# Attention projections of six units per block as seven products of halves

## The chip, the cores and the metric

The kernel runs on one core of a Trainium2 chip. The core has a matrix engine (TensorE; PE in the profile, with PEld for its weight loads), VectorE (DVE), ScalarE (ACT), GpSimd (POOL), and SyncE (SP), whose queue issues the transfers between the device memory and the core's SBUF. Matmuls write to eight banks of PSUM. The metric is the device time of one execution in microseconds.

## The reference

Thirty-two sequences of 64 positions with 512 features, in fp32, go through two layers. Each is conditioned by its own row of `cond`. Cut to what matters:

```python
# layer 0: 8 query heads of 64, one key/value head
h = ada_rms(x, cond, ln1_w, ln1_tw)              # normed, scaled per sequence
q, k = rope(h @ Wq.T), rope(h @ Wk.T);  v = h @ Wv.T
x = x + softmax(q @ k.T / 8) @ v @ Wo.T          # Wq, Wo: 512 x 512
h = ada_rms(x, cond, ln2_w, ln2_tw)
x = x + (silu(h @ Wg.T) * (h @ Wu.T)) @ Wd.T     # 512 -> 2048 -> 512
# layer 1: 16 query heads of 32, four key/value heads from a latent of 128
h = ada_layernorm(x, cond, W_ada, b_ada)
q = rope(h @ Wq.T);  c = h @ Wkd.T;  k, v = rope(c @ Wku.T), c @ Wvu.T
x = x + softmax(q @ k.T / sqrt(32)) @ v @ Wo.T   # Wq, Wo: 512 x 512
```

The mask of layer 1 hides nothing at 64 positions.

## The kernel before

The 2,048 positions are cut into eight units of 256 (four sequences). Everything is kept transposed: features on the partitions, positions along the columns, so a unit of `x` is four chunks of 128 features by 256 positions. There are three kinds of work for a unit: `attention0`, `mlp` and `attention1`.

The MLP already multiplies by halves: a 256x256 block of weights times a 256x256 block of a unit, cut in two both ways, takes seven products of halves in place of eight (Strassen's scheme in Winograd's form, P1 to P7). `first_products` makes P1, P6, P5, P7 in the four parts of a PSUM bank; VectorE and ScalarE read them into sums; `last_products` makes P2, P3, P4 over parts of the same bank. A set of weights holds seven 128x256 pieces, three quarters of the weights and four sums (`set`, 896 KB). The sums are made in unit 0 (`combine`, L250) and stored to device memory (`kept`); later units load both parts (L242 and L247) into a ring of five sets. The loads are issued when the last products of a set have been emitted (`done_with`).

The attention projections are whole products. `project` (L523) runs over the four chunks: a unit's queries or outputs are 4 x 4 multiplications of 128 features by 256 positions. In both blocks `query(0)` and `query(1)` make two chunks each and `rotate` (L527) applies the positional rotation straight from PSUM; `output` (L564) projects the contexts `cT` and VectorE adds the result to `x` (L573). Their weights (`wqkv`, `wo0`, `wq1`, `wo1`) stay in SBUF throughout, in the fixed area of 14,103 columns (`STAY`).

Two pools of PSUM matter: attention has two banks ("at"), the MLP two for gate and up ("gu") and four for down.

The order of the work is made in two steps. A planner (`Order`, L67) emits pieces of generators: each piece yields its PE cost and a latency before its successor may come, and the job with the smallest share done goes first. During the MLP of unit u run `attention0` of unit u + 1 and, from unit 1 on, a chain of `attention1` of earlier units (`behind`, L1058). The framework then places each engine's instructions by readiness, with that order as priority; so instructions of different pieces are interleaved, and each engine's order is fixed when the program is built. Units 0 and 1 of block 0, and 6 and 7 of block 1 (at the end), run with `lean`, a variant with less latency; the other six units of each block do not.

Of the kernel before, what the change touches and what calls it, by code (L numbers as in the profile page):

```python
# [17 lines left out]
P = 128  # L18
# [29 lines left out]
STAY = 14103  # L48
# [60 lines left out]
def two_blocks(ctx: ExitStack, tc: tile.TileContext, a: dict, out: bass.AP):  # L109
# [115 lines left out]


# [38 lines left out]

    mods = []
# [16 lines left out]
    for i, w in enumerate(wqkv):  # L283
        nc.sync.dma_start(w, a[f"wqkv{i}"])
# [238 lines left out]
    def project(ps, w, cols, h):  # L523
        for k in range(KC):
            nc.tensor.matmul(ps, w[:, k, cols], h[:, k, :], start=(k == 0), stop=(k == KC - 1))  # L525

    def rotate(dst, src, cos, sin, shape, name):  # L527
# [7 lines left out]
        nc.vector.stream_shuffle(v, v, OTHER)  # L535
        nc.gpsimd.tensor_tensor(dst, u, v, ALU.add)  # L536
# [27 lines left out]
    def output(u, cT, w, name, last=False):  # L564

        x = x_units[u]
        for h in range(2):
# [12 lines left out]
    def attention0(u, room, early=None, late=None):  # L580
# [4 lines left out]
        def query(i):  # L585

            q = abank(f"q0_{u}_{i}").rearrange("p (c t) -> p c t", c=2)
            for c in range(2):
                project(q[:, c], wqkv[i], slice(c * P, (c + 1) * P), h)
# [8 lines left out]
        def keys_values():  # L598
            kv = abank(f"kv0_{u}")
            project(kv[:, :UT], wqkv[0], slice(2 * P, 3 * P), h)  # L600
            return kv

        norm = rms(u, s0a, h, room, f"a{u}")
        yield next(norm)
# [19 lines left out]
        turn = turn or query(0)  # L624
        turn(cos, sin)
        yield 0.0 if lean else 3.4, 0.0
# [22 lines left out]
        query(1)(cos, sin)  # L649
        yield 3.4, 0.0  # L650
# [14 lines left out]
        for ts in ((0,), (1,)) if lean else ((0, 1),):  # L665
# [16 lines left out]
            yield 0.5 * len(ts), 5.0 * ts[0] if lean else 10.0  # L682
# [56 lines left out]
        yield 0.43, 0.0  # L739


    def attention1(u, room):
# [6 lines left out]
        else:  # L749
# [4 lines left out]
            yield 0.0, 6.0  # L754
            mean = mean_of([total], f"mean_{u}")
        sq = tile4(room, "h", f"sq1_{u}") if lean else work("sq", [P, KC, UT], f"sq1_{u}", 1)
        for part in (slice(0, 2), slice(2, 4)) if lean else (slice(0, 4),):
# [3 lines left out]
            nc.scalar.activation(sq[:, part], h[:, part], AF.Square)  # L761
        parts = [sq[:, k] for k in range(KC)] if lean else [total_of(room, sq, f"v{u}")]
# [7 lines left out]
        for part in (slice(0, 2), slice(2, 4)) if lean else (slice(0, 4),):  # L770
# [7 lines left out]
        project(lat[:, :UT], wkd, slice(0, LAT), h)  # L778
# [7 lines left out]
        def query(i):  # L786
            q = abank(f"q1_{u}_{i}")
            for c in range(2):
                project(q[:, c * UT : (c + 1) * UT], wq1, slice((2 * i + c) * P, (2 * i + c + 1) * P), h)
# [10 lines left out]
        query(0)  # L800
        yield 3.4, 0.0
# [31 lines left out]
        query(1)  # L833
        yield 3.4, 4.5
# [24 lines left out]
        def context(t, ps):  # L859
# [19 lines left out]
            yield 1.0, 1.5 * t  # L879
# [315 lines left out]
```

## Time and profile before

| What | Value |
|---|---|
| median of 3 runs | 1057.65 us (1056.87 to 1057.7) |
| the profiled execution | 1055.26 us, of which span 1053.4 us |
| granted PE clock over the span | 0.989 |
| PE busy, PE weight loads busy | 96%, 89% |
| VectorE, ScalarE, GpSimd busy | 52%, 31%, 41% |
| moved by DMA | 198.55 MB, 188 GB/s in the mean |
| query projections, records of 256 columns (L525 `q`) | 512 |
| output projections (L525 `po`) | 512 |
| gate and up products of 128 columns (L899) | 3584 |

The profile is one execution with the hardware profiler. Instructions are grouped by line, engine and tile names (buffer numbers left out); the chain of work follows the end of the program back to what released each step. Matmuls are pipelined and their ends are modelled, so durations of single matmuls overlap; the distance from one to the next is read from the chain.

### The profile page before, as it was taken

To read this page: it belongs to the slowest core of one execution; us is meant where nothing else is said; L and a number is where in the kernel's file an instruction comes from. 1 tells how busy PE (TensorE), PEld (TensorE's weight loads), DVE (VectorE), ACT (ScalarE), POOL (GpSimd) and SP (SyncE) were. 2 spreads that over 40 slices of the span, in tenths; PEclk is the share of its full clock that TensorE was granted. 3 is DMA by queue.
4 is the path that set the end of the run, shared out by engine and by line. 5 is a ranking of instruction groups with operands and counts; after the bars stand their busy time and mean duration, and the time that the engine had idled before them with its cause. 6 is when DMAs were issued, how large, how long until landed. Compare 5 with 4: busy or idle time off the path is not lost.

```text
span 1053.4 us, 21591 instructions
## 1 busy us (share of the span) xinstructions
PE 1012.6 (96%) x8602; PEld 938.7 (89%) x8602; DVE 546.7 (52%) x1377; ACT 329.1 (31%) x680; POOL 432.8 (41%) x518
## 2 busy tenths in 40 slices
PE   7899999999999999999999999999999999999887
PEld 6679999998999889989999989999999899999765
DVE  4966646545355385353555286532655345352363
ACT  4342112255114243142431332341424422141132
POOL 3424545443255443355341544234632335432541
PEclk8989999999999999999999999999999999999899
DMA  8816896463666364663555565465735547564001
GB/s 277 310 61 218 288 303 247 151 211 122 234 210 211 108 244 152 219 243 127 212 178 181 207 209 183 141 214 187 277 117 194 202 165 280 204 229 170 11 1 40
DMA packets 68275, 198.55 MB, mean 188 GB/s; under 512 B 7248, under 2 KB 15184, under 8 KB 67792
## 3 DMA queue, kind: packets, MB, share of 16 engines
q1 hardware_dynamic: 68176, 197.17, 53.4%
q8 instruction: 69, 1.13, 0.4%
q14 instruction: 30, 0.25, 0.1%
HBM read 180.37 MB, written 16.78 MB: 187 GB/s over the span
## 4 chain that ended last, share of the span: by engine, by line
PE 81%; DVE 8%; POOL 5%; DMA 2%; issue 2%; ACT 1%; SPq 0%; ACTq 0%; POOLq 0%; DVEq 0%
PE gu L899 34%; PE down L958 17%; PE po L525 10%; PE q L525 9%; DMA set<-in_wmlp 2%; PE cx L869 2%; PE sc L845 1%; PE lat L525 1%; PE pp L560 1%; PE sc L673 1%; PE kv L525 1%; PE cx L694 1%; DVE sm L553 1%; PE tab L400 1%; DVE mx L545 1%
## 5 line engine op out<-in xcount | busy, mean ns | idle before, releaser
L899 PE MATMUL gu<-h,set 128*128 128x128 f32 x2048 | 288.1, 277 | 6.4 <-DVE c L918 5.7
L899 PEld LDWEIGHTS gu<-h,set 128*128 128x128 f32 x2048 | 258.8, 192 | 15.5 <-issue 10.4
L899 PE MATMUL gu<-hc,set 128*128 128x128 f32 x1536 | 215.2, 275 | 0.0
L899 PEld LDWEIGHTS gu<-hc,set 128*128 128x128 f32 x1536 | 193.5, 192 | 1.0 <-issue 0.6
L937 POOL TENSOR_TENSOR act<-c,c 128x384 f32<-128x384 f32 x64 | 66.4, 1038 | 210.5 <-DVE c L925 140.8
L958 PE MATMUL down<-td,set 128*128 128x128 f32 x1024 | 137.5, 276 | 3.3 <-POOL td L940 2.5
L958 PEld LDWEIGHTS down<-td,set 128*128 128x128 f32 x1024 | 125.4, 192 | 5.2 <-POOL td L940 3.5
L911 ACT COPY e<-gu 128x128 f32<-128x128 f32 x128 | 33.7, 264 | 259.9 <-PE gu L899 246.8
L525 PE MATMUL q<-h,stays 128*128 128x256 f32 x480 | 111.3, 385 | 1.5 <-POOL h L774 1.5
L525 PE MATMUL po<-cT,stays 128*128 128x256 f32 x480 | 109.0, 382 | 2.1 <-DVE sm L553 2.1
L958 PE MATMUL down<-act,set 128*128 128x128 f32 x768 | 109.5, 278 | 0.0
L925 DVE TENSOR_TENSOR c<-gu,u 128x256 f32<-128x256 f32 x128 | 53.4, 419 | 106.4 <-PE gu L899 106.1
L525 PEld LDWEIGHTS q<-h,stays 128*128 128x128 f32 x480 | 90.9, 193 | 14.3 <-POOL h L774 1.7
L525 PEld LDWEIGHTS po<-cT,stays 128*128 128x128 f32 x480 | 89.8, 191 | 14.0 <-ACT cT L878 2.6
L958 PEld LDWEIGHTS down<-act,set 128*128 128x128 f32 x768 | 97.6, 192 | 5.2 <-issue 3.2
L913 DVE TENSOR_TENSOR u<-e,gu 128x128 f32<-128x128 f32 x128 | 35.9, 281 | 127.5 <-ACT e L911 126.8
L555 POOL TENSOR_TENSOR p<-p,sm 128x512 f32<-128x512 f32 x40 | 41.6, 1058 | 121.4 <-DVE sm L554 113.7
L536 POOL TENSOR_TENSOR qT<-u_q,v_q 128x512 f32<-128x512 f32 x30 | 38.1, 1269 | 97.2 <-DVE v_q L535 97.1
L573 DVE TENSOR_TENSOR x<-x,po 128x512 f32<-128x512 f32 x32 | 22.0, 687 | 87.7 <-PE po L525 87.7
L994 ACT ACT_TABLE_LOAD x34 | 43.6, 1283 | 54.5 <-DVE c L925 54.0
L939 POOL TENSOR_TENSOR td<-act 128x256 f32<-128x256 f32 x64 | 46.7, 730 | 5.6 <-DVE act L936 0.9
L994 ACT ACTIVATE c<-gu 128x128 f32<-128x128 f32 x64 | 17.7, 277 | 90.2 <-DVE c L925 82.2
(269 smaller groups left out, 1333.0 us busy)
## 6 DMA issues: line engine op xcount, KB each, us to landing
set<-sums SPq DMA_DIRECT2D x168, 512.0 KB, 5.6
set<-in_wmlp SPq DMA_DIRECT2D x192, 384.0 KB, 4.6
sums<-set SPq DMA_DIRECT2D x24, 512.0 KB, 4.1
x<-in_x SPq DMA_DIRECT2D x8, 512.0 KB, 5.5
out_x<-x SPq DMA_DIRECT2D x16, 256.0 KB, 2.3
mod<-in_mod SPq DMA_DIRECT2D x7, 512.0 KB, 5.2
a<-in_wmlp SPq DMA_DIRECT2D x24, 128.0 KB, 3.1
stays<-in_wo SPq DMA_DIRECT2D x2, 1024.0 KB, 8.0
```

The source lines that it names most:

```text
L525: nc.tensor.matmul(ps, w[:, k, cols], h[:, k, :], start=(k == 0), stop=(k == KC - 1))
L536: nc.gpsimd.tensor_tensor(dst, u, v, ALU.add)
L555: nc.gpsimd.tensor_tensor(p8, p8, sm.unsqueeze(2).to_broadcast(wide), ALU.mult)
L573: nc.vector.tensor_tensor(x[:, part], x[:, part], po, ALU.add)
L899: nc.tensor.matmul(ps, w[:, slot, k * P : (k + 1) * P], b[of][:, k], start=start and k == 0, stop=k == 1, skip_group_check=True)
L911: nc.scalar.copy(e, ps[:, 0])
L913: nc.vector.tensor_tensor(u2, e, ps[:, 1], ALU.add)
L925: nc.vector.tensor_tensor(c.rearrange("p (a b) t -> p a b t", b=2)[:, :, 1], ps[:, 2:4], u2.unsqueeze(1).to_broadcast([P, 2, HT]), ALU.add,)
L937: nc.gpsimd.tensor_tensor(act[:, 1:4], gate[:, 1:4], c[:, 1:4], ALU.mult)
L939: nc.gpsimd.tensor_tensor(td[:, 0:2], act[:, 1:3], act[:, 0:2], ALU.subtract)
L958: nc.tensor.matmul(sums_of[u][p][:, c], w[:, slot, c * P : (c + 1) * P], b[of], start=q % NP == 0 and i % 2 == 0 and c == 0, stop=q % NP = ...
L994: nc.scalar.activation(gate[2][:, 0], gate[0][:, 0], AF.Silu)
```

## The change

Non-lean units, six in each block, make their query and output projections by seven products of halves. `load_asets` loads a pair of sets per projection (`wattn`, `akept`), two rings of two, one for each block; the next pair is asked for where the last projection has been emitted. In the first unit of each block `combine_asets` makes the four weight sums of each set and stores them. `sums_in` makes the four sums of the input on VectorE: for queries as soon as the norm has made `h`, for outputs just ahead of the products. `in_halves` makes the products of both sets, evacuates them into `c` in SBUF, and leaves the rest to `rotate`, or to GpSimd, which adds `c` to `x`. Lean units keep the whole products: the first two from tiles that are dropped afterwards, the last two from weights loaded ahead of the last unit's MLP into the tiles of block 0's ring. Some costs and latencies that the planner is given change with it.

```diff
-STAY = 14103
+STAY = 5911
...
-    wqkv = [fixed([P, KC, 384]), fixed([P, KC, 256])]
-    wo0 = fixed([P, KC, D])
-    wq1 = fixed([P, KC, D])
+    wkv0 = fixed([P, KC, P])
+    wq0 = [work("wq0", [P, KC, 2 * P], f"wq0_{i}") for i in range(2)]
+    wo0 = work("wo", [P, KC, D], "wo0", 1)
     wkd = fixed([P, KC, LAT])
     wkv1 = fixed([P, 2, P])
-    wo1 = fixed([P, KC, D])
+    whole1 = []
...
+    def by_chunk(w):
+        return [w[:, k] for k in range(KC)]
+    def product(ps, p, w, b, start=False, stop=False):
+        slot, of = OF[p]
+        for k in range(2):
+            nc.tensor.matmul(
+                ps, w[:, slot, k * P : (k + 1) * P], b[of][:, k], start=start and k == 0, stop=k == 1, skip_group_check=True
+            )
...
+    akept = [dram.tile([P, 4, 2 * P], F32, tag=f"asums{i}", name=f"asums{i}") for i in range(8)]
+    asets = {b: {"n": 0, "now": [], "odd": [], "units": 6} for b in range(2)}
+    def load_asets(block):
+        s_ = asets[block]
+        n = s_["n"]
+        if n == 2 * s_["units"]:
+            return
+        s_["n"], s_["now"], s_["odd"] = n + 1, [], []
+        for i in range(2):
+            j = 4 * block + 2 * (n % 2) + i
+            t = work(f"aw{block}", [P, 7, 2 * P], f"aset{block}_{n}_{i}", 2)
+            nc.sync.dma_start(t[:, 4:7], a["wattn"][j][:, 0:3])
+            if n < 2:
+                s_["odd"].append(work("a21", [P, 2 * P], f"aa21_{block}_{n}_{i}", 2))
+                nc.sync.dma_start(s_["odd"][-1], a["wattn"][j][:, 3])
+            else:
+                nc.sync.dma_start(t[:, 0:4], akept[j])
+            s_["now"].append(t)
+    def combine_asets(block):
+        s_ = asets[block]
+        for i, a21 in enumerate(s_["odd"]):
+            t = s_["now"][i]
+            nc.vector.tensor_tensor(t[:, 0], a21, t[:, 6], ALU.add)
+            nc.vector.tensor_tensor(t[:, 1], t[:, 0], t[:, 4], ALU.subtract)
+            nc.vector.tensor_tensor(t[:, 2], t[:, 4], a21, ALU.subtract)
+            nc.gpsimd.tensor_tensor(t[:, 3], t[:, 5], t[:, 1], ALU.subtract)
+            nc.sync.dma_start(akept[4 * block + 2 * ((s_["n"] - 1) % 2) + i], t[:, 0:4])
+        s_["odd"] = []
+    def sums_in(block, h, name):
+        t = work(f"as{block}", [P, 4, 2, HT], f"as_{name}", 1)
+        b11, b12, b21, b22 = (h[:, r_, c_] for r_ in (slice(0, 2), slice(2, 4)) for c_ in (slice(0, HT), slice(HT, UT)))
+        nc.vector.tensor_tensor(t[:, 0], b12, b11, ALU.subtract)
+        nc.vector.tensor_tensor(t[:, 2], b22, b12, ALU.subtract)
+        nc.vector.tensor_tensor(t[:, 1], b22, t[:, 0], ALU.subtract)
+        nc.vector.tensor_tensor(t[:, 3], b21, t[:, 1], ALU.subtract)
+        return {"B11": b11, "B21": b21, "B22": b22, "T1": t[:, 0], "T2": t[:, 1], "T3": t[:, 2], "T4": t[:, 3]}
+    def in_halves(block, b, name):
+        some = []
+        for i, w in enumerate(asets[block]["now"]):
+            ps = abank(f"ha_{name}_{i}").rearrange("p (r t) -> p r t", t=HT)
+            for j, p in enumerate(("P1", "P6", "P5", "P7")):
+                product(ps[:, j], p, w, b, start=j == 0)
+            e = work("ea", [P, HT], f"ea_{name}_{i}")
+            nc.scalar.copy(e, ps[:, 0])
+            u2 = work("u2a", [P, HT], f"u2a_{name}_{i}")
+            nc.vector.tensor_tensor(u2, e, ps[:, 1], ALU.add)
+            w2 = work("w2a", [P, HT], f"w2a_{name}_{i}")
+            nc.vector.tensor_tensor(w2, u2, ps[:, 2], ALU.add)
+            c = work("ca", [P, 4, HT], f"ca_{name}_{i}")
+            nc.vector.tensor_tensor(c[:, 3], w2, ps[:, 3], ALU.add)
+            some.append((w, ps, u2, c))
+        for w, ps, u2, c in some:
+            for j, p in ((0, "P2"), (2, "P3"), (3, "P4")):
+                product(ps[:, j], p, w, b, stop=p == "P4")
+            nc.scalar.copy(c[:, 0], ps[:, 0])
+            nc.vector.tensor_tensor(c[:, 1:3], ps[:, 2:4], u2.unsqueeze(1).to_broadcast([P, 2, HT]), ALU.add)
+        return [c.rearrange("p (r c) t -> p r (c t)", r=2) for _, _, _, c in some]
+    def pair_of(t, i):
+        return t.rearrange("p (r i) t -> p i r t", r=2)[:, i]
...
-    for i, w in enumerate(wqkv):
-        nc.sync.dma_start(w, a[f"wqkv{i}"])
+    nc.sync.dma_start(wkv0, a["wkv0"])
+    for i, w in enumerate(wq0):
+        nc.sync.dma_start(w, a[f"wq0{i}"])
...
-            nc.tensor.matmul(ps, w[:, k, cols], h[:, k, :], start=(k == 0), stop=(k == KC - 1))
+            nc.tensor.matmul(ps, w[k][:, cols], h[:, k, :], start=(k == 0), stop=(k == KC - 1))
...
+        if list(dst.shape) != list(u.shape):
+            u, v = (t.rearrange("p (r b) s -> p r (b s)", r=2) for t in (u, v))
         nc.gpsimd.tensor_tensor(dst, u, v, ALU.add)
...
     def output(u, cT, w, name, last=False):
 
         x = x_units[u]
+        if w is None:
+            block = int(last)
+            for i, c in enumerate(in_halves(block, sums_in(block, cT, f"o{name}"), f"o{name}")):
+                nc.gpsimd.tensor_tensor(pair_of(x, i), pair_of(x, i), c, ALU.add)
+                if last:
+                    nc.sync.dma_start(pair_of(out[u], i), pair_of(x, i))
+            yield 6.3, 2.0
+            return
...
-        yield next(norm)
+        at_first = next(norm)
+        if not lean:
+            combine_asets(0)
+            h_sums = sums_in(0, h, f"q0_{u}")
+        yield at_first
...
-        turn = turn or query(0)
-        turn(cos, sin)
-        yield 0.0 if lean else 3.4, 0.0
+        if lean:
+            turn(cos, sin)
+            yield 0.0, 0.0
...
-        query(1)(cos, sin)
-        yield 3.4, 0.0
+        if lean:
+            query(1)(cos, sin)
+            yield 3.4, 0.0
+        else:
+            two = [P, 2, UT]
+            for i, c in enumerate(in_halves(0, h_sums, f"q0_{u}")):
+                rotate(
+                    pair_of(qT, i), c, *(t.unsqueeze(1).to_broadcast(two) for t in (cos, sin)), two, f"q0_{u}_{i}"
+                )
+            yield 6.3, 0.0
+            load_asets(0)
...
-            yield 0.5 * len(ts), 5.0 * ts[0] if lean else 10.0
+            yield 0.5 * len(ts), 5.0 * ts[0] if lean else 12.5
+        if not lean:
+            combine_asets(0)
...
             contexts([0, 1])
-            yield 1.1, 2.5
-        yield from output(u, cT, wo0, f"0_{u}")
+            yield 1.1, 4.0
+        yield from output(u, cT, by_chunk(wo0) if lean else None, f"0_{u}")
...
         if late:
             late()
         yield 0.43, 0.0
+        if not lean:
+            load_asets(0)
...
             yield 0.0, 6.0
+            if u:
+                load_asets(1)
...
             nc.scalar.activation(sq[:, part], h[:, part], AF.Square)
+        if not lean:
+            combine_asets(1)
...
             nc.gpsimd.tensor_tensor(by_seq(h[:, part]), by_seq(h[:, part]), per_seq(t1, u)[:, part], ALU.add)
+        if not lean:
+            h_sums = sums_in(1, h, f"q1_{u}")
         yield 0.43, 5.5 if lean else 9.0
...
-        query(1)
-        yield 3.4, 4.5
+        if lean:
+            query(1)
+            yield 3.4, 4.5
+        else:
+            many = [P, 2 * US, S]
+            for i, c in enumerate(in_halves(1, h_sums, f"q1_{u}")):
+                rotate(
+                    pair_of(qT, i),
+                    c.rearrange("p r (b s) -> p (r b) s", s=S),
+                    cos.unsqueeze(1).to_broadcast(many),
+                    sin.unsqueeze(1).to_broadcast(many),
+                    many,
+                    f"q1_{u}_{i}",
+                )
+            yield 6.3, 4.5
+            load_asets(1)
...
-            yield 1.0, 1.5 * t
+            yield 1.0, 1.5 * t if lean else 3.5 * t
...
-            yield 0.9, (0.0, 6.0)[t] if lean else 9.0
+            yield 0.9, (0.0, 6.0)[t] if lean else 11.5
             if not lean:
+                combine_asets(1)
                 yield from context(t, ps[t])
...
-        yield from output(u, cT, wo1, f"1_{u}", True)
+        yield from output(u, cT, whole1[1] if lean else None, f"1_{u}", True)
...
-    for w, key in ((wq1, "wq1"), (wkd, "wkd"), (wkv1, "wkv1"), (wo1, "wo1")):
+    for w, key in ((wkd, "wkd"), (wkv1, "wkv1")):
         nc.sync.dma_start(w, a[key])
...
         if u == 1:
             jobs.append(chain)
+            load_asets(0)
+            load_asets(1)
+        if u == NU - 1:
+            rest_of = work("as0", [P, 2, D], "last_chunks", 1)
+            for i, key in enumerate(("wq1", "wo1")):
+                w = work("aw0", [P, 7, 2 * P], key, 2).rearrange("p a b -> p (a b)")[:, : 3 * D]
+                w = w.rearrange("p (k d) -> p k d", d=D)
+                nc.sync.dma_start(w, a[key][:, :3])
+                nc.sync.dma_start(rest_of[:, i], a[key][:, 3])
+                whole1.append([w[:, k] for k in range(3)] + [rest_of[:, i]])
...
-        "wqkv0": _lay(np.concatenate([wq0[:256], wk0, i["L0_cond_Wv"]], 0)),
-        "wqkv1": _lay(wq0[256:]),
+        "wkv0": _lay(np.concatenate([wk0, i["L0_cond_Wv"]], 0)),
+        "wq00": _lay(wq0[:256]),
+        "wq01": _lay(wq0[256:]),
+        "wattn": np.concatenate([_quarters(w, False) for w in (wq0, i["L0_cond_Wo"], wq1, wo1)], 0),
```

`product` is moved up, not changed.

More of the change, by code (lines that the diff above doesn't have):

```diff
@@ L588, in query @@
             for c in range(2):
-                project(q[:, c], wqkv[i], slice(c * P, (c + 1) * P), h)
+                project(q[:, c], by_chunk(wq0[i]), slice(c * P, (c + 1) * P), h)
             two = [P, 2, UT]
@@ L599, in keys_values @@
             kv = abank(f"kv0_{u}")
-            project(kv[:, :UT], wqkv[0], slice(2 * P, 3 * P), h)
+            project(kv[:, :UT], by_chunk(wkv0), slice(0, P), h)
             return kv
         norm = rms(u, s0a, h, room, f"a{u}")
-        yield next(norm)
+        at_first = next(norm)
[3 more added lines that the diff above has]
+        yield at_first
         if early:
@@ L774, in attention1 @@
             nc.gpsimd.tensor_tensor(by_seq(h[:, part]), by_seq(h[:, part]), per_seq(t1, u)[:, part], ALU.add)
+        if not lean:
+            h_sums = sums_in(1, h, f"q1_{u}")
         yield 0.43, 5.5 if lean else 9.0
         lat = abank(f"lat_{u}")
-        project(lat[:, :UT], wkd, slice(0, LAT), h)
+        project(lat[:, :UT], by_chunk(wkd), slice(0, LAT), h)
         latT = space(room, "latT", UT, f"latT_{u}")
@@ L788, in query @@
             for c in range(2):
-                project(q[:, c * UT : (c + 1) * UT], wq1, slice((2 * i + c) * P, (2 * i + c + 1) * P), h)
+                project(q[:, c * UT : (c + 1) * UT], whole1[0], slice((2 * i + c) * P, (2 * i + c + 1) * P), h)
             many = [P, 2 * US, S]
@@ L798, in query @@
             )
-        query(0)
-        yield 3.4, 0.0
+        if lean:
+            query(0)
+            yield 3.4, 0.0
         kv = abank(f"kv1_{u}")
@@ L831, in attention1 @@
         yield 0.9, 0.0
-        query(1)
-        yield 3.4, 4.5
+        if lean:
+            query(1)
[13 more added lines that the diff above has]
+            load_asets(1)
         cT = tile4(room, "h", f"cT1_{u}")
@@ L890, in attention1 @@
             yield from context(1, ps[1])
-        yield from output(u, cT, wo1, f"1_{u}", True)
+        yield from output(u, cT, whole1[1] if lean else None, f"1_{u}", True)
     finished = set()
     acts = {}
-    def product(ps, p, w, b, start=False, stop=False):
-        slot, of = OF[p]
-        for k in range(2):
-            nc.tensor.matmul(
-                ps, w[:, slot, k * P : (k + 1) * P], b[of][:, k], start=start and k == 0, stop=k == 1, skip_group_check=True
-            )
     def first_products(m, q):
@@ L1127, in _quarters @@
     else:
-        q = w.reshape(2, NP, P, 2, 2, P).transpose(1, 5, 0, 3, 4, 2)
-    return q.reshape(NP, P, 4, 2 * P)[:, :, [0, 1, 3, 2]]
+        q = w.reshape(2, -1, P, 2, 2, P).transpose(1, 5, 0, 3, 4, 2)
+    return q.reshape(-1, P, 4, 2 * P)[:, :, [0, 1, 3, 2]]
 def _column(v):
```

## The prediction

> **What bounds the kernel now.** I read the head of the page first, to see which engine is full.
>
> ```profile
> span 1053.4 us, 21591 instructions
> PE 1012.6 (96%) x8602; PEld 938.7 (89%) x8602; DVE 546.7 (52%) x1377; ACT 329.1 (31%) x680; POOL 432.8 (41%) x518
> ```
>
> TensorE is. Its busy time alone proves little, so I asked for the long middle of the program, 140 to 940 us, where all the changed work lies (the columns are PE, PEld, DVE, ACT, POOL busy, clock, DMA share, GB/s):
>
> ```profile
> 140.00:940.00 800.00, 790.47 (x6672) 743.48 (x6674) 405.65 (x1016) 255.95 (x512) 336.71 (x392) 1.00 0.57 199
> ```
>
> PE lacks work for only 9.5 us of 800, at full clock. So whatever leaves PE there leaves the time, unless a new wait takes its place. What a matmul costs is read from the chain of work in order of time, where pipelined matmuls stand without their overlap:
>
> ```profile
> 302.91 2.68 PE gu L899 x24
> 310.82 3.57 PE gu L899 x32
> ...
> 330.93 3.45 PE q L525 x16
> ```
>
> The multiplications are fp32 and each appears as two records. A record with 256 columns takes 3.45 / 16 = 0.216 us, one with 128 columns 2.68 / 24 = 0.1116 us (the piece of 32 gives the same).
>
> Next, what PE waits for in that middle (us, times, longest), and three stretches where another resource is at its fullest (columns as above):
>
> ```profile
> PE gu L899 <- DVE c L918: 4.1, 4, 1.8
> PE pp L560 <- POOL p L555: 2.7, 2, 1.9
> ```
>
> ```profile
> 150.00:200.00 50.00, 50.00 (x391) 48.24 (x391) 26.98 (x67) 13.27 (x26) 24.42 (x30) 1.00 0.73 257
> 376.00:396.00 20.00, 17.40 (x169) 16.23 (x168) 17.55 (x48) 7.47 (x14) 6.61 (x8) 1.00 0.57 198
> 615.00:635.00 20.00, 19.49 (x141) 18.30 (x141) 18.82 (x53) 3.96 (x11) 7.42 (x10) 1.00 0.50 173
> ```
>
> No DMA is among the waits. At a DMA share of 0.73 PE lost nothing. Where VectorE is 88 to 94% busy (two turns from one unit to the next, when the angles are computed as well) PE lost 2.6 and 0.5 us in 20. VectorE is the next engine to watch. The rows for costing it, by shape, and the DMA rows (KB each, median us to landing):
>
> ```profile
> L925 DVE TENSOR_TENSOR c<-gu,u 128x256 f32<-128x256 f32 x128 | 53.4, 419 | 106.4 <-PE gu L899 106.1
> L573 DVE TENSOR_TENSOR x<-x,po 128x512 f32<-128x512 f32 x32 | 22.0, 687 | 87.7 <-PE po L525 87.7
> L732 DVE TENSOR_TENSOR hc<-h 128x256 f32<-128x256 f32 x8 | 4.6, 571 | 0.1
> L734 DVE TENSOR_TENSOR hc<-h,hc 128x256 f32<-128x256 f32 x8 | 3.9, 481 | 0.0
> ```
>
> ```profile
> set<-sums SPq DMA_DIRECT2D x168, 512.0 KB, 5.6
> set<-in_wmlp SPq DMA_DIRECT2D x192, 384.0 KB, 4.6
> ```
>
> **What the Trainium skill says.** "TensorE: Matmul & The Clock Gate", section Back-to-back issue gap, gives a matmul a gap that grows with its columns plus a small fixed part; so halving the columns should not quite halve the time. The trace agrees: 0.1116 against 0.216 / 2 = 0.108 us. "SBUF — State Buffer", section Who interferes with whom, says that a VectorE instruction with two SBUF inputs contends with a GpSimd instruction that reads SBUF, and one with a PSUM input does not. The trace agrees: the same 128x256 subtraction took 419 ns with an input in PSUM and 571 and 481 ns in L732 and L734 with both in SBUF. "DMA: Bandwidth & Descriptors", section Issuing engines are not separate DMA queues, says that all transfers share the same 16 engines; so new loads delay those of the MLP. No run here has the new loads yet.
>
> **The change part by part.**
>
> *PE.* A projection of one unit was 16 multiplications of 256 columns, 32 records: 32 x 0.216 = 6.92 us. Seven products, two chunks, two output sets: 28 of 128 columns, 56 records: 56 x 0.1116 = 6.25 us. Saved 0.67 us. Four projections (queries and outputs in two blocks), six units: 24 x 0.67 = 16.1 us less PE work. There are 24 x 24 more weight loads, but the 128-column pitch was measured with one load to each record, so it contains them. This gain is nearly certain; the rest is what comes against it.
>
> *VectorE.* Per projection `sums_in` adds four 128x256 operations with both inputs in SBUF (571 + 450 + 481 + 415 ns in L732 to L735): 1.92 us, 46 us for 24. Per set of products three evacuations of 128x128 (281 + 284 + 285 ns, L913 to L918) and one of 128x256 (419): 1.27 us, 61 us for 48 sets. The outputs lose two additions of 687 ns: 24 x 0.687 = 16.5 us off. The rotation now reads `c` in SBUF rather than PSUM; at the 25% by which L732 to L734 exceed 419 ns this is up to 48 x 0.17 = 8 us. `combine_asets` once for eight sets: 8 x 1.64 = 13 us. Together some 111 us: VectorE goes from 405.65 of 800 (51%) to about 65% in the middle. *ScalarE* gets 96 copies of 264 ns, 25 us. *GpSimd* gets 24 additions of 1.06 to 1.27 us to `x` and eight subtractions of 0.82 us, 32 to 37 us: 42% to 46%. None becomes full, so none sets the end as a sum; they count only through waits of PE.
>
> *PE's waits on the evacuations.* In the MLP, other pieces lie between the first four products of a bank and the last three, which overwrite its parts. In `in_halves` only the other set's 16 records (1.8 us) lie between, and P6 needs a sum that VectorE makes just before. In exchange the order on the queues is made from readiness: in the trace a query's 16 records lie between two gate records, so a later MLP piece can be put in front of a late product. Eight sets per unit join sixteen of the MLP, half as many again. The middle's 9.5 us of loss times one half is 4.8; with the shorter cover I take +6 us. Bounds: -2 (the new order may also close gaps that exist now) and +28 (the rival below). Behind a waiting product on PE's queue stand the MLP's gate and down matmuls, and so ScalarE's `e` and the rest; there is nothing else to take up the wait.
>
> *DMA.* Each projection's pair of sets is 2 x 896 KB. At the 343 GB/s that the window 580 to 585 us moved, that is a burst of 5.3 us, 24 times; in all some 41 MB loaded and 4 MB stored on top of 198.55. In the middle 199 GB/s become about 250, a share near 0.72, which the window at 0.73 carried at no loss. What can hurt is the burst ahead of an MLP set, since SP's queue is one and an aset's load is issued as soon as its projection is done. From issue, landing and first matmul of each set I took the slack: gate and up sets land a median 10.4 and 11.1 us before use, down sets 5.0 us (least 1.0), and 32 of 57 down sets have under 5.3 us. Laying a burst behind the end of each of 23 projections in this trace, a set is both in its shadow and short of slack twice, at 637 and 911 us: 1.9 + 2.2. I take +4 us; bounds 0 and, with every second burst in front of a down set at 2.5 us, +30. The sets themselves have long cover: from a block's queries to its outputs lie scores, softmax and context.
>
> *First sums.* In unit 1 four `a21` tiles share a ring of two, so SP's queue stands until VectorE has combined the first pair, with the MLP's loads behind it; SP waited 8.7 us in two waits for L257 in this way already. Five MLP sets are ahead. I take +1.5 us, bounds 0 and 7.
>
> *Start and end.* `wq1` and `wo1` no longer load at 44 us; the DMA share then falls to 0.00 from 60 to 70 us, so nothing waited behind them: 0, and 0 too if that cover goes, as PE then works on unit 0. They load ahead of the last unit, whose 120 us hide 2 MB. The two tail units keep the whole products. The outputs' store has pieces of 1 KB rather than 2 KB; only units 0 to 5, off the end. More tiles than before share SBUF (8,192 columns freed, some 11,000 asked for, beside early ones that die); a wait for room would show with the VectorE rival.
>
> Sum: -16.1 + 6 + 4 + 1.5 = -4.6 us. The profiled execution took 1055.26 us (span 1053.4, so 1.9 outside) and would take 1050.7. The median of the runs is 2.4 above it: 1057.65 - 4.6 = 1053 us.
>
> **The rivals.**
>
> *VectorE turns into the bound at the turns between units* (the other side). The window 376 to 396 has 17.55 of 20 us of VectorE work. If a query's sums and evacuations (about 5.1 us) fall into it, they do not fit, and MLP, softmax and angles behind them are late. Six turns, 4 us lost at each, with 2 us more at the two with angles, is 28 us, in place of my 6: -16.1 + 28 + 5.5 = +17.4, so 1075; at half that loss +3.4, so 1061. It decides from (16.1 - 5.5) / 6 = 1.8 us lost per turn, where the gain is gone. For it: 65% mean load, 1.75 us reciprocals in the same queue, and new instructions whose inputs both lie in SBUF. Against it: 500 to 550 us was 62% VectorE with 49.98 of 50 us of PE. Taken at its middle, 1068.
>
> *The bursts hit the down sets.* If the order puts MLP behind most projections, as it must while attention waits for softmax, 12 bursts cost 2.5 us: +30, giving about 1079. For it the 32 of 57; against it the two hits of 23.
>
> *Even.* Waits eat the gain: 1057.65.
>
> **How the numbers follow.** Faster as summed 0.47; VectorE 0.30; bursts 0.11; even, within 0.2% (2.1 us, about what a measurement of this kernel can tell from no change), 0.12. So faster 0.47, same 0.12, slower 0.41. The likeliest case alone reaches from 1043 (waits at -2 and little of the rest) to 1055.5. The range goes on to 1075, which holds most of the VectorE case and some of the bursts.
>
> **What would show it.** Right: PE busy in the middle falls by some 16 us; products of 128 columns keep 0.1116 us each; VectorE near 65%; DMA near 0.72 and no DMA in the chain after unit 1; PE's idle time in the middle between 15 and 25 us for the same stages. Wrong: idle above 28 us, waits of `ha` on `as` or `u2a`, or of `gu` and `down` on VectorE; a DMA of `set` in front of `down`; or a pitch of 0.1236 us, at which 56 records cost the 6.92 us that the 32 did.

## The result and the profile after

The change makes the kernel slower: 1092.82 us in the median of four runs (1091.83 to 1093.58) against 1057.64, a ratio of 1.0332 with a 95% interval from 1.0316 to 1.0347. The forecast was 1053 us with 1075 as its upper end, so both the sign and the range missed.

First the head of the page of after (its profiled execution took 1091.83 us) and the window from 140 to 940 us, with the columns that the prediction showed:

```profile
span 1090.0 us, 23227 instructions
PE 1011.0 (93%) x9178; PEld 952.5 (87%) x9178; DVE 673.6 (62%) x1665; ACT 351.8 (32%) x775; POOL 479.0 (44%) x550
```

```profile
140.00:940.00 800.00, 752.21 (x6873) 720.92 (x6871) 513.86 (x1251) 267.91 (x581) 367.08 (x405) 0.99 0.68 243
```

PE now stands idle for 47.8 of these 800 us, where it was 9.5. VectorE is at 64% and the DMA share is 0.68. Next, what PE waits for in that window (us in total, times, longest):

```profile
PE gu L233 <- DVE c L1042: 7.8, 10, 1.7
PE down L1082 <- POOL td L1064: 6.4, 5, 4.5
PE ha_o L233 <- DVE as_o L316: 5.7, 2, 3.2
PE ha_q L233 <- DVE ca_q L335: 5.5, 5, 4.1
PE pp L644 <- POOL p L639: 4.8, 2, 3.2
```

Two of the five are waits of the new products, for a sum and for an evacuation. The other three existed before and have grown: those of the gate products from 4.1 us, of the transposition of the probabilities (`pp`) from 2.7, both shown in the prediction, and of the down products from this:

```profile
PE down L958 <- POOL td L940: 1.3, 4, 0.5
```

Again no DMA is among them.

To balance the books I took all matmul records from the first gate product of unit 1 to the last down product. The pitch is the usual distance from the start of one record to that of the next (0.1116 us at 128 columns, 0.216 at 256). Lost time is what the distance has beyond the pitch, wherever that is over 0.12 us. Of the time outside it in which PE's clock was halved, one half counts as lost to the clock.

| us | stretch | lost | half clock | PE's work (rest) |
|---|---|---|---|---|
| before | 825.2 | 13.3 | 0 | 812.0 |
| after | 860.4 | 56.9 | 12.2 / 2 = 6.1 | 797.4 |
| difference | +35.2 | +43.6 | +6.1 | -14.6 |

The stretch holds nearly the whole 36.6 us by which the span grew. PE's work fell as forecast; waits took three times that back. By the engine that ended the wait, the lost time is VectorE 30.5 us (before 4.8), GpSimd 13.8 (7.0), ScalarE 7.4 (1.0).

The three stretches that the prediction looked at, in after:

```profile
150.00:200.00 50.00, 48.23 (x416) 46.49 (x415) 38.26 (x93) 13.74 (x29) 26.66 (x32) 1.00 0.93 331
376.00:396.00 20.00, 18.61 (x184) 17.64 (x186) 13.54 (x34) 9.37 (x17) 11.76 (x15) 1.00 0.80 298
615.00:635.00 20.00, 17.80 (x151) 16.79 (x144) 13.68 (x29) 8.64 (x17) 9.40 (x8) 1.00 0.41 145
```

The reader should see how little a load says: with VectorE at 77% and DMA at 0.93, PE lost 1.8 of 50 us; with VectorE at 68% and DMA at 0.41 it lost 2.2 of 20.

The VectorE rows, by shape, which answer L732 to L735 and L913 to L925 of before:

```profile
L616 DVE TENSOR_TENSOR u_q<-ca_q,stays 128x512 f32<-128x512 f32 x12 | 14.7, 1223 | 0.0
L316 DVE TENSOR_TENSOR as_q<-h,as_q 128x256 f32<-128x256 f32 x12 | 11.3, 943 | 0.0
L341 DVE TENSOR_TENSOR ca_q<-ha_q,u2a_q 128x256 f32<-128x256 f32 x24 | 10.1, 420 | 9.6 <-ACT ca_q L340 9.6
L330 DVE TENSOR_TENSOR u2a_q<-ea_q,ha_q 128x128 f32<-128x128 f32 x24 | 6.8, 284 | 14.8 <-ACT ea_q L328 14.8
```

The evacuations, which read a bank, cost what was priced (284 and 420 ns). The instructions whose inputs both lie in SBUF do not. The view of single tiles gives shortest, median and longest in ns:

```profile
L316 DVE TENSOR_TENSOR as_q<-h,as_q x11: 414/672/2131, 205.9 to 914.8; 128x256 f32<-128x256 f32 x11
```

The same subtraction takes 0.41 us or 2.13. The Trainium skill's page "SBUF — State Buffer", section Who interferes with whom, says that a VectorE instruction with two SBUF inputs contends with a GpSimd instruction that reads SBUF, and calls their shared ports an exclusive lock. The trace agrees: the subtraction of 2.13 us began 0.13 us after GpSimd's `h` of L594, and ended 0.3 us after it.

```profile
247.05 1.98 POOL L594 TENSOR_TENSOR h<-x,stays 128x1024 f32<-128x1024 f32 x1
247.18 2.13 DVE L316 TENSOR_TENSOR as_q<-h,as_q 128x256 f32<-128x256 f32 x1
```

It is no single case. Of the 96 input sums and 48 rotation multiplications from SBUF in the trace of after, 51 took over 1.25 times the usual 0.415 or 0.685 us, and each of these 51 overlapped with a GpSimd instruction. All 144 together took 43.5 us more than at the usual times. The rotation meets GpSimd by its own structure. Timeline of the second half of a query (start, duration, then engine and line):

```profile
223.07 0.68 DVE L615 TENSOR_TENSOR v_q<-ca_q,stays 128x512 f32<-128x512 f32 x1
223.31 1.56 POOL L620 TENSOR_TENSOR qT<-u_q,v_q 128x512 f32<-128x512 f32 x1 [3.40 <-DVE v_q L617]
223.66 1.77 DVE L616 TENSOR_TENSOR u_q<-ca_q,stays 128x512 f32<-128x512 f32 x1
```

GpSimd adds the first half of the query while VectorE multiplies the second, now from SBUF: 1.77 us in place of 0.68. The change puts the two halves back to back, so 12 of the 24 multiplications of L616 took over 1.2 us.

One place shows how the pieces add up. This is the chain of work from 358 to 370 us (start, duration, what):

```profile
358.40 1.85 DVE sign L416
...
361.25 0.30 DVE ang L420
361.57 0.29 DVE ang L421
361.86 0.34 DVE as_o L314
362.20 0.40 DVE u L1037 x2
362.59 0.40 DVE w L1039 x2
362.99 0.40 DVE c L1042 x2
363.38 0.34 DVE as_o L315
363.72 0.35 DVE as_o L316
364.07 0.04 issue
364.11 6.14 PE ha_o L233 x38
```

The products of an output waited for a sum of the context. That sum stood behind the angles' instructions; one of these (L416), on 128x128, took 1.84 us while GpSimd made `h` for 1.91; the same instruction took 0.22 us in the mean before. Then six evacuations of the MLP went between the first and the second of the four sums, because the order was fixed so. PE stood for 3.17 us; and the 38 records after that took 0.162 us each, not 0.1116, since PE's clock was halved for 3.41 us from 364.86 on.

### The profile page after: what moved, and what is told of

Its sections match the earlier page's. It is cut to its first block, busy times and chain, and to the rows that moved or that the text cites. A ratio compares the mean times of both kernels' runs of the same rounds, so it can differ in the third digit from the quotient of the medians.

```text
span 1090.0 us, 23227 instructions
## 1 busy us (share of the span) xinstructions
PE 1011.0 (93%) x9178; PEld 952.5 (87%) x9178; DVE 673.6 (62%) x1665; ACT 351.8 (32%) x775; POOL 479.0 (44%) x550
## 4 chain that ended last, share of the span: by engine, by line
PE 61%; DVE 22%; POOL 5%; DMA 5%; ACT 3%; issue 3%; SPq 0%; ACTq 0%; POOLq 0%; DVEq 0%
PE gu L233 26%; PE down L1082 12%; PE ha_o L233 6%; PE ha_q L233 4%; DMA set<-in_wmlp 3%; PE po L607 3%; DVE u_q L616 2%; PE cx L999 2%; DVE v_q L615 1%; DVE v_q L617 1%; PE pp L644 1%; PE sc L975 1%; PE q L607 1%; PE lat L607 1%; DVE mx L629 1%
## 5 line engine op out<-in xcount | busy, mean ns | idle before, releaser
L233 PE MATMUL gu<-h,set 128*128 128x128 f32 x2048 | 291.5, 278 | 16.9 <-DVE c L1042 9.8
L1082 PE MATMUL down<-td,set 128*128 128x128 f32 x1024 | 140.5, 278 | 7.9 <-POOL td L1064 7.6
L620 POOL TENSOR_TENSOR qT<-u_q,v_q 128x512 f32<-128x512 f32 x30 | 42.2, 1406 | 86.3 <-DVE v_q L617 86.3
L654 POOL TENSOR_TENSOR x<-x,ca_o 128x512 f32<-128x512 f32 x24 | 31.1, 1297 | 63.6 <-DVE ca_o L341 63.5
L233 PE MATMUL ha_o<-as_o,aset 128*128 128x128 f32 x384 | 53.0, 284 | 5.7 <-DVE as_o L316 5.7
L233 PEld LDWEIGHTS ha_o<-as_o,aset 128*128 128x128 f32 x384 | 49.0, 201 | 6.1 <-DVE as_o L316 6.1
L233 PE MATMUL ha_q<-as_q,aset 128*128 128x128 f32 x384 | 51.4, 277 | 0.0
L233 PE MATMUL ha_q<-h,aset 128*128 128x128 f32 x288 | 41.9, 283 | 6.2 <-DVE ca_q L335 5.5
L233 PEld LDWEIGHTS ha_q<-as_q,aset 128*128 128x128 f32 x384 | 47.4, 194 | 0.0
```

Of the source, the lines that this page charges most:

```text
L233: nc.tensor.matmul(ps, w[:, slot, k * P : (k + 1) * P], b[of][:, k], start=start and k == 0, stop=k == 1, skip_group_check=True)
L654: nc.gpsimd.tensor_tensor(pair_of(x, i), pair_of(x, i), c, ALU.add)
L1082: nc.tensor.matmul(sums_of[u][p][:, c], w[:, slot, c * P : (c + 1) * P], b[of], start=q % NP == 0 and i % 2 == 0 and c == 0, stop=q % NP = ...
```

## The experiments

My theory after the result: the work beside TensorE (sums, evacuations, rotation from SBUF, additions on GpSimd) makes VectorE and GpSimd late for PE. Rivals: the loads; the order of work, which differs in every kernel; scarce room in SBUF; and VectorE's load as such. All ratios are to the kernel before with its own planner figure, 27, run beside. A run marked "figure 26" has another order of the same work; it is to be compared with another run of figure 26, and the kernel before with that figure is c1.

| run | median us | ratio, 95% interval |
|---|---|---|
| e1, no reloads | 1103.24 | 1.0433 [1.0385, 1.0482] |
| c0, figure 26 | 1102.04 | 1.0411 [1.0364, 1.0458] |
| e3, figure 26, evacuations on ScalarE | 1089.01 | 1.0303 [1.0262, 1.0343] |
| e2, figure 26, no sums | 1075.19 | 1.0165 [1.0134, 1.0196] |
| e4, figure 26, e3 and no sums | 1067.34 | 1.0093 [1.0056, 1.0129] |
| e6, bare products | 1050.08 | 0.993 [0.9904, 0.9956] |
| e6b, bare, figure 26 | 1052.30 | 0.9962 [0.9947, 0.9977] |
| c1, before, figure 26 | 1071.71 | 1.0151 [1.0135, 1.0166] |
| e10, figure 26, no sums for queries | 1081.83 | 1.0214 [1.0175, 1.0254] |
| e9, figure 26, queries not evacuated | 1078.45 | 1.0191 [1.0164, 1.0218] |
| e7, outputs alone | 1059.65 | 1.0019 [1.0008, 1.0031] |
| e11, e7 with the addition on VectorE | 1055.51 | 0.9992 [0.998, 1.0003] |
| e8, before with idle sums | 1064.89 | 1.0075 [1.0047, 1.0104] |
| e12, before, rotation from SBUF | 1056.15 | 0.9987 [0.9977, 0.9998] |
| e13, before with less room | 1057.69 | 1.0011 [0.9997, 1.0024] |
| e14, e11 with old latencies | 1054.83 | 0.9981 [0.9971, 0.9991] |
| e16, e11, figure 26 | 1067.93 | 1.0105 [1.0084, 1.0127] |
| e15, e16 for block 1 alone | 1068.32 | 1.0104 [1.0078, 1.0131] |

Nine of the eighteen times lie outside all that was expected of them: e1, c0, c1 and e15 above, e2 and e6b below, and e3, e4 and e6 between two ranges. The order of the work alone, by c0 and c1, can move a time by as much as most of these misses.

### The loads

```diff
-        if n == 2 * s_["units"]:
+        if n >= 2:
             return
```

> The attention sets are loaded for the first unit of each block only; all later units multiply by the pair that is there, so their queries and outputs are made with the wrong weights, at the same instructions on TensorE, VectorE, ScalarE and GpSimd. About 36 MB of loads in 20 bursts are gone. If the bursts are the cause, some 36 us go and the time is near 1057 or below. If VectorE is the cause (its sums and evacuations late, TensorE waiting for them), the time stays within 1087 to 1093 us and TensorE's losses in the middle stay above 45 us.

```profile
140.00:940.00 800.00, 750.90 (x6797) 718.85 (x6798) 509.77 (x1238) 267.07 (x577) 361.34 (x396) 0.98 0.56 200
```

The DMA share of the window fell from 0.68 to 0.56, below the 0.57 of before. PE stood idle in it for 49.1 us, against 47.8 in after, and the time rose by 10 us. The loads are not the cause. Without them the same instructions stand in another order on every engine; I put the rise down to that, and c0 shows how much an order can do.

### Sums and evacuations

The kernels e2, e3 and e4, and the others so marked in the table, have a planner figure of 26 rather than 27. It is the total that the planner takes for `attention0`. So c0 is the change with that figure, and their reference:

```diff
-    A0, A1, M = 27.0, 24.0, 74.0
+    A0, A1, M = 26.0, 24.0, 74.0
```

> The changed kernel with one figure of the planner altered (the cost of attention of block 0 taken as 26 rather than 27), as the reference for the two kernels that follow, which have the same figure. It makes another order of the same instructions. Both theories: 1085 to 1100 us; what it differs from 1092.8 is what an order alone is worth.

No operation of the change is another, only their order, and the time rose by 9 us. That is a warning for all single comparisons below some 10 us, and below 15 when c1 is counted. e3 then takes the evacuations off VectorE:

```diff
-            nc.vector.tensor_tensor(u2, e, ps[:, 1], ALU.add)
+            nc.scalar.copy(u2, ps[:, 1])
...
-            nc.vector.tensor_tensor(c[:, 1:3], ps[:, 2:4], u2.unsqueeze(1).to_broadcast([P, 2, HT]), ALU.add)
+            nc.scalar.copy(c[:, 1:3], ps[:, 2:4])
```

> Planner figure 26. The evacuations of the products are made by ScalarE as plain copies of the same parts in the same places, without the additions (so the results are wrong); VectorE loses 61 us, ScalarE gains about as much; sums of the input stay on VectorE. If VectorE's lateness is the cause: 1065 to 1078 us. If bursts or the two banks that a projection holds are the cause: within 5 us of the reference with figure 26.

e2 leaves the four input sums out, and e4 does both:

```diff
-        nc.vector.tensor_tensor(t[:, 0], b12, b11, ALU.subtract)
...
-        return {"B11": b11, "B21": b21, "B22": b22, "T1": t[:, 0], "T2": t[:, 1], "T3": t[:, 2], "T4": t[:, 3]}
+        return {"B11": b11, "B21": b21, "B22": b22, "T1": b12, "T2": b22, "T3": b12, "T4": b21}
```

> Planner figure 26, reference 1102.0 us. The four sums of the input are left out (the products read the plain quarters, so the results are wrong); the evacuations stay on VectorE. VectorE loses four operations per projection, 50 to 70 us with their waits for GpSimd. If VectorE is the cause and the sums are one half of it: 1080 to 1088 us. If the evacuations alone are the cause: above 1096 us.

> Planner figure 26. As the kernel before it, and the four sums of the input are left out too (the products read the plain quarters instead, so the results are wrong): VectorE's load is then about that of the kernel without the change, while TensorE's products and the loads of the sets are all there. If VectorE is the cause: 1040 to 1055 us, the 16 us of TensorE's work now showing. If bursts are the cause: above 1075 us.

Against c0, e3 gains 13 us, e2 27 us and e4 35 us. So the sums matter, which the prediction had put down at their busy time alone; of the evacuations e3 tells less, since they are still made, on ScalarE. Against the kernel before in the same order (c1, 1.0151), e2 at 1.0165 is level: without its sums the change neither gains nor loses. And e4, whose VectorE is nearly as free as before (560.2 us busy against 546.7), is 0.6% faster than c1, some 6 us, where PE has 17 us less work. What PE of e4 waits for, same window:

```profile
PE pp L638 <- POOL p L633: 7.1, 5, 2.9
PE down L1076 <- POOL td L1058: 6.4, 4, 3.5
PE gu L233 <- DVE c L1036: 4.7, 6, 1.7
```

GpSimd stands at the head of it: 18.1 of the 39.4 us that e4 lost in the stretch are its, against 8.6 in c1, which is before with the same figure. So VectorE is not the only late engine. e6 therefore takes all of the new work away, and leaves products, loads and banks. The sums are left out as in e2, the rotation reads the bank, and VectorE rather than GpSimd adds to `x`, as in the kernel before:

```diff
...
-            nc.scalar.copy(c[:, 0], ps[:, 0])
-            nc.vector.tensor_tensor(c[:, 1:3], ps[:, 2:4], u2.unsqueeze(1).to_broadcast([P, 2, HT]), ALU.add)
-        return [c.rearrange("p (r c) t -> p r (c t)", r=2) for _, _, _, c in some]
+        return [ps.rearrange("p (r c) t -> p r (c t)", r=2) for _, ps in some]
...
-                nc.gpsimd.tensor_tensor(pair_of(x, i), pair_of(x, i), c, ALU.add)
+                nc.vector.tensor_tensor(pair_of(x, i), pair_of(x, i), c, ALU.add)
```

> Planner figure 27, reference 1092.8 us. Products, sets, loads and banks are those of the changed kernel, but no sums are made, nothing is evacuated into c, and rotation and addition to x read the bank straight, as in the kernel before (the results are wrong). Work on VectorE, ScalarE and GpSimd is then that of the kernel before. If the side work is the whole cause: 1038 to 1046 us, the 16 us of TensorE's work gained. If the form of the products is to blame (two banks at once, their order, the loads): above 1060 us.

e6 is 43 us below after, with the same figure 27. The window of e6, and two of its products in the chain of work:

```profile
140.00:940.00 800.00, 784.37 (x7286) 756.18 (x7286) 428.82 (x1050) 260.51 (x519) 346.67 (x403) 1.00 0.72 257
```

```profile
209.75 6.25 PE ha_q L233 x56
227.47 6.25 PE ha_o L233 x56
```

56 records in 6.25 us are the price in the prediction. The DMA share is the predicted 0.72 with every load made, and PE lost only 17.8 us in the stretch: this clears the loads and the products together. Bare products gain 7 us, short of the forecast 16 even so. In their profiled execution, 4.5 us below that of before, PE's work is 17.6 us less, but 4.5 us more are lost to waits, 3.4 to half clock, and 5 us lie at the start and the end.

### Does it hold in another order?

> The kernel before with the planner figure 26 in place of 27; no instruction differs, only the order. The figure cost 9 us with the change and 12 us with the outputs alone. If it costs these because VectorE is fuller there: before loses under 4 us, 1055 to 1061 us. If the order of figure 26 is worse for every kernel: 1065 to 1071 us, and then 26 is to be compared with 26 and the change costs about as much there, 31 to 37 us.

> e6 (products only: input sums and evacuations left out, rotation and the addition to x read the bank) with the planner figure 26. If the work beside TensorE is the cause in any order: 35 to 45 us below c0, 1057 to 1067 us. If the 43 us between after and e6 were largely luck of one order: under 25 us below c0, above 1077 us.

The kernel before loses 15 us by the figure 26 alone (c1), with no engine fuller. The figure costs the change 9 us and the bare products 2, so its price differs from kernel to kernel. Compared within 26, the change costs 1.0411 / 1.0151 = 1.0256, 27 us, and the bare products gain 1.9%, 20 us; they lie 50 us below c0. So with both figures the change is some 27 to 35 us slower than before, and its bare products faster. The side work is the cause in both; its exact price is not to be had from one order.

### Queries or outputs?

e7 makes the outputs alone by seven products, with sets that stay in SBUF; queries are whole again:

```diff
-        if n == 2 * s_["units"]:
+        if n == 1:
             return
...
-            h_sums = sums_in(0, h, f"q0_{u}")
...
+        query(1)(cos, sin)
+        yield 3.4, 0.0
```

> Planner figure 27. Seven products for the outputs alone; the queries are whole products as before, with their weights kept, and the outputs' two sets per block are made once and stay in SBUF (no reload). If every projection costs alike: half of the 35 us, 1070 to 1078 us. If the outputs are worse, because their sums are made just ahead of the products: 1080 to 1090 us. If the queries are worse (sums waiting for GpSimd's h, rotation with both inputs in SBUF): 1055 to 1066 us.

e11 adds `c` to `x` on VectorE:

```diff
-                nc.gpsimd.tensor_tensor(pair_of(x, i), pair_of(x, i), c, ALU.add)
+                nc.vector.tensor_tensor(pair_of(x, i), pair_of(x, i), c, ALU.add)
```

> Outputs alone by seven products, as in the run with outputs only (1059.65 us), and VectorE rather than GpSimd adds c to x; the results are the reference's. If GpSimd's queue is what is left to lose there (12.5 us of waits): 1050 to 1056 us, the first version below the kernel before. If VectorE's is: 1060 to 1066 us.

The outputs alone are even. From e7 to after are 33 us, from e11 to after 37, from e16 to c0, both with 26, 34 us: the queries carry nearly all of the loss. These kernels also load no set again, which e1 clears, and leave more room in SBUF, of which below. The addition on GpSimd is worth 4 us of it, if the order allows to say so.

Of the queries, e10 leaves the sums of `h` out, and e9 keeps the sums and lets the rotation read the bank:

```diff
+        if name[0] == "q":
+            return {"B11": b11, "B21": b21, "B22": b22, "T1": b12, "T2": b22, "T3": b12, "T4": b21}
```

```diff
+            if straight:
+                some.append((w, ps, None, ps))
+                continue
```

> Planner figure 26, reference 1102.0 us. Of the queries alone the four sums of h are left out (plain quarters instead, so the queries are wrong); the evacuation, the rotation and the outputs are as in the change. If the sums of h, queued on VectorE behind GpSimd's h and contending with GpSimd, are the cause: 1076 to 1086 us, as with no sums at all. If the rotation is: 1093 to 1102 us.

> Planner figure 26, reference 1102.0 us. Of the queries alone the evacuation into c is left out: the rotation reads the bank straight, as in the kernel before (the queries are wrong). The sums of h stay, the outputs are as in the change. If the queries' evacuation and the rotation with both inputs in SBUF are the cause: 1075 to 1085 us. If the sums of h are: 1095 to 1102 us.

They give back 20 and 24 us of c0. Together that is more than the 34 us that the queries cost, as it must be if the two lengthen each other, though part of it may be order. In e9 the row of `u_q` is back at 679 to 681 ns, from 1176 to 1223 in after.

### The single costs by themselves

e8 puts 24 groups of four sums, which nobody reads, into the kernel before:

```diff
+        nc.vector.tensor_tensor(t[:, 0], b12, b11, ALU.subtract)
+        nc.vector.tensor_tensor(t[:, 2], b22, b12, ALU.subtract)
+        nc.vector.tensor_tensor(t[:, 1], b22, t[:, 0], ALU.subtract)
+        nc.vector.tensor_tensor(t[:, 3], b21, t[:, 1], ALU.subtract)
```

> The kernel before (whole products), with the 24 groups of four sums made on VectorE at the same places and used by nobody. If VectorE's queue is what is lost, because the MLP's evacuations come behind the sums: 1064 to 1075 us. If it is only that TensorE waits for the new sums and evacuations themselves: 1055 to 1060 us.

8 us, for 42 us of VectorE that no product waits for. In the profiles PE's instructions stand in the order of before up to the record 5,112 of 8,602, and at that point 5.1 of the 9.4 us by which the span is longer are there already: this much is not due to another order on PE. One wait shows a part of it; it had 4.1 us before:

```profile
PE gu L914 <- DVE c L933: 6.6, 6, 1.7
```

So a load in VectorE's queue delays the MLP's evacuations even with half of the engine free. e12 gives the kernel before the change's other new pair, a copy on ScalarE and a rotation from SBUF:

```diff
+            held = work("ca", [P, 512], f"ca_{name}").rearrange("p (c t) -> p c t", t=shape[2])
+            nc.scalar.copy(held, src)
+            src = held
```

> The kernel before (whole products), where ScalarE copies the queries of six units per block into SBUF and the rotation reads them there. If two inputs in SBUF beside GpSimd are costly by themselves: rotations of 0.8 to 1.2 us rather than 0.68 to 0.69, and 1062 to 1072 us. If it is only a longer row that PE does not wait for: 1055 to 1060 us.

Nothing is lost: `u_q` takes 684 and 862 ns in the mean, and over 1.2 us in 3 of 24, since the halves of a query lie apart there. The sums by themselves took 431 to 586 ns on `h` in e8, where they take 733 to 943 in after. Each part is cheaper alone than in the change. By the measure used above, 28 of the 144 sums and multiplications of e8 and e12 were lengthened beside GpSimd, where 51 of 144 are in after. That they meet GpSimd more often there is read from the traces, and that they lengthen each other is argued from it; no run takes GpSimd's share of it away alone.

### Room in SBUF

At 643.8 us of after a product waited 4.14 us for an evacuation (L335), which waited for GpSimd's `kb`, a tile that it doesn't read. e13 takes 2,048 columns of SBUF from the kernel before:

```diff
-STAY = 14103
+STAY = 16151
```

> The kernel before, with 2,048 columns of SBUF set aside in the fixed area and used by nobody, so that working tiles have about as much less room as the change leaves them; nothing else. In the trace of after, one product waited 4.14 us for an evacuation that itself waited for GpSimd's kb, on which its inputs do not depend: the tile's place was still in use. If such waits for room are a part of the loss: slower by 5 to 15 us, 1062 to 1072 us. If the lateness of VectorE and GpSimd alone makes it: within 2 us of before, 1055 to 1059 us.

No effect in the kernel before, whose instructions kept their order on all four engines. Whether the change, with more tiles alive at once, pays for room remains open.

### The outputs alone, with other latencies and another order

> Outputs by seven products with resident sets, VectorE adds c to x, queries whole (as e11), and the four latencies that the planner is given for scores and contexts put back to those of before. The PE gain of about 10.6 us stays in e11 and 9 us of waits plus half clock eat it. If these waits come of the order that the longer latencies make: 1048 to 1053 us, a version that beats both. If they come of the outputs' own sums and evacuations: 1054 to 1059 us.

> e11 (outputs alone, VectorE adds c to x) with the planner figure 26 in place of 27: no instruction differs, only the order. For the whole change this figure was worth 9 us. If the order's share goes with how full VectorE is, it is smaller here: 1053 to 1060 us. If it is a matter of the order alone: off by 5 us or more either way, below 1050.5 or above 1060.5 us.

> As e16 (outputs with resident sets, VectorE adds c to x, planner figure 26), but for block 1 alone; block 0 projects its outputs whole. Six projections of the twelve: half of the gain of PE, 4 to 5 us, and half of the sums and evacuations. If the loss grows more than linearly with VectorE's work: below e16 and below before, 1050 to 1055 us. If the loss is in proportion or comes of the order: 1056 to 1062 us.

The edit of e14 is four of the planner's latencies:

```diff
-            yield 0.5 * len(ts), 5.0 * ts[0] if lean else 12.5
+            yield 0.5 * len(ts), 5.0 * ts[0] if lean else 10.0
```

and so 4.0 to 2.5, 3.5 to 1.5, 11.5 to 9.0. At 1054.83 us, 0.19% below before with an interval that excludes 1, e14 is the fastest version that leaves nothing out. But 2 us are at the edge of what a measurement tells from no change: e12, which only adds work to the kernel before, came out 0.13% below it, and its interval excludes 1 as well. PE's work in the profile of e14 is 7.4 us less, 7.4 us more are lost and 1.7 go to half clock. Putting the latencies back gave 0.7 us from e11, within the range put down for waits that come of the outputs' own sums and evacuations; and one wait for such a sum holds most of the loss:

```profile
PE ha_o L234 <- DVE as_o L316: 6.5, 4, 2.5
```

e15 kept the block 0 outputs whole and is level with e16, so half of the outputs do not pay more than all. With 26, e15 and e16 are both faster than c1, by 0.5%, some 5 us.

## Why the prediction was wrong

- **PE: right.** The forecast was 16.1 us less work; the stretch shows 14.6, and 17.6 in the bare products, at the pitch that was read from the chain.
- **DMA: inside its bounds, too high.** +4 us were put down. No load is among PE's waits in the window of after, and in that of e6, which makes every load, one of 0.2 us. The +1.5 us for the first sums can't be told apart in the runs.
- **VectorE's load: right in the window by luck, and of no use.** 64% against a forecast 65%. Over the whole program it grew by 127 us, not 111; the longer program thinned it out. The sums cost more than the 1.92 us of a projection: the four rows add to 3.43 us for queries and 2.35 for outputs. The rotation's instructions grew by 14 us, not 8. The evidence for contention was thinner than the prediction says: L925 is an addition, not the same subtraction, and L735, with both inputs in SBUF, took 415 ns, no more than L925.
- **The waits: the step that failed.** "With the shorter cover I take +6 us" measured +43.6 us, and +6.1 of half clock that the sum had no term for. I scaled the loss that was there, 9.5 us, by the number of evacuated sets, as if losses added up in proportion. e11 (+61 us of VectorE) lost 9 us more than before, and after (+127 us) 44. The term also had in view only the evacuations, and left the sums at their busy time; the runs of figure 26 show the sums as the greatest single part (by the ratios, e2 lies 26 us below c0, and c1 27). As the chain at 358 us shows, a product cannot go on without its sum, and the sum stands behind whatever VectorE has in its queue.
- **The bound: too low.** +28 came from six turns between units at 4 us and the angles. In the 25 us ahead of each of the six later starts of an MLP lie only 9.7 of the 56.9 us lost, and in 30 us 21. The rival with VectorE as the bound had the right engine; most of the loss lies in other places, and it had no GpSimd, which holds 13.8 us.
- **"None becomes full, so none sets the end as a sum" is where the choice went wrong.** It is true and proves nothing: VectorE is 62% busy and makes PE lose 30.5 us. The window at 500 to 550 us of before, at 62% with no loss, had been no evidence for the new work, whose products wait for it directly. The same window of before and of after, where VectorE is as busy and PE loses 5.5 us:

```profile
500.00:550.00 50.00, 49.98 (x447) 46.72 (x446) 30.76 (x77) 20.59 (x38) 20.93 (x27) 1.00 0.53 186
500.00:550.00 50.00, 44.54 (x418) 42.20 (x417) 30.72 (x73) 18.34 (x35) 22.72 (x26) 1.00 0.58 213
```

- Of the signs named as "wrong" those of the VectorE case came: idle above 28 us, `ha` on `as`, `gu` on VectorE. `down` waited mostly for GpSimd rather than VectorE. Those of the other cases, a load in front of `down` and a pitch of 0.1236 us, did not.

## What to carry to other kernels

When side work is put around products on a full engine, count for each product how many instructions of another engine must end before it and what those may stand behind, not the mean load of that engine; here a mean of 62% went with 30.5 us of waits for it. Where a product waits for an instruction with two SBUF inputs, look also at its longest case (here 2.13 against 0.41 us) when GpSimd is busy beside it, and expect costs that are small alone to add up to more than their sum. Before a change of a few per cent is laid to its instructions, try the same instructions in a second order: here one planner figure moved the kernel before by 15 us.

## What was not expected of the hardware

PE's clock halves for 3.4 us, or twice that, during a wait or just after it, in the midst of a program that keeps it 93% busy. In the stretch of after there are four such windows, 17.1 us together, of which 12.2 fall on products. The Trainium skill's page "TensorE: Matmul & The Clock Gate", part The HAM clock gate, says that half rate comes after an idle window of about 3.4 us, and that the windows run free of the program. The length and the rate agree. The threshold does not: a gap of 1.74 us in e8 and one of 1.95 in e1 had such a window 0.8 and 1.2 us after its end, and nothing longer was near. Nor does a longer gap always bring one: those of 3.24 us in after (at 530) and 2.81 in e10 had none. Before, with no gap over 1.93 us, had no window in the stretch. So by these lengths (half of 3.4 us) a wait of some 2 us may cost an estimated 1.7 us more than it lasts, and its length alone does not tell which one does.
